# A woven attention loop: the order of TensorE's work written out link by link

## The chip, the cores and the metric

The kernel runs on one core of a Trainium2 chip. The metric is the device time of one execution in microseconds, as the median of several runs. The core has engines that run side by side and synchronise by semaphores: PE (TensorE, matmuls), DVE (VectorE), ACT (ScalarE), POOL (GpSimd) and SP (SyncE, which here only issues DMAs). Each engine works through its own queue in order.

## The reference

Two layers act on `x` of shape (2, 1024, 512). Only the first layer's attention is touched by the change.

```python
xn = layernorm(x)
q, k, v = (silu(causal_dwconv(xn @ W, taps, bias)) for each of q, k, v)   # 16 heads of 128
k = k / sqrt(128)
alpha, beta = sigmoid(xn @ Wa + ba), sigmoid(xn @ Wb + bb)                # one each per head and step
def step(S, (q, k, v, alpha, beta)):                                      # S is 128 x 128 per head
    err = S k - v
    S = alpha * S - beta * err k^T
    return S, S q
o = layernorm(scan(step)) * ln_w + ln_b
s = (o * sigmoid(xn @ Wg)) @ Wo
x = x + s * silu(mlp(xn))
```

The second layer (a gated linear recurrence beside an MLP with 4-bit weights) follows in the same program and is not changed.

## The kernel before, in words

The recurrence is done in chunks of 128 steps. There are 8 groups of two heads (`hg`), and with the batch of 2 a group has `NS` = 4 independent streams. A group has 8 chunks (`c`), taken in pairs (`p`, 256 steps) for the projections.

Inside a chunk the recurrence is a triangular system. Its matrix L comes from k k^T and from the decays; the running sum of the log decays is called g. The system is solved in four blocks of 32 rows, whose diagonal blocks are inverted beforehand.

The first stretch of the program, called the front here, holds a layernorm of `x`, the first layer's MLP (`mlp`, a generator that hands out its work in pieces by `some(n)`), the decays, and for group 0 everything that must be ready ahead of the loop. Then comes the attention loop over groups, pairs and chunks; then the join (`Join`, which multiplies with `Wo`); then the second layer.

The functions of the loop are these:

- `project` does one product with a 512 x 256 weight block: two halves of four 128x512 matmuls each, into PSUM tiles `pwq`, `pwk` or `pwv` of a pool with two buffers. ACT copies each half into `pre` and writes a scaled copy into the destination, DVE adds three taps of the convolution, ACT applies silu.
- `ahead` prepares one pair of the **next** group: the k product, the decay matrix `e` (a DMA that broadcasts rows of g from `gr`, a mask on DVE, four exps on ACT) and k k^T (`pkk`), which DVE multiplies into L (`lt`). k, e and L go to DRAM.
- `invert` inverts the diagonal blocks of the next group in 31 dependent pairs of DVE instructions (`tl`, `ml`); it is a generator too.
- `within` fetches what a chunk needs (L into `ground`, `eb`, and rows of g into `eg`, of which ACT takes the exp), multiplies k and q with it on POOL (`kg`, `qg`), and forms `at` and `kd` from two PE products (`pqk`, and the transpose `pk`).
- `across` is the chain of a chunk. Its links in order: `pks` (state times k) on PE, `rt` on DVE, the transpose `pr` on PE, `rr` on ACT; then four times `pw` on PE, `w4` on ACT, `pz` on PE, `rr` on DVE; then `wt`, the state's product `pst`, the new state on DVE, and the output `po`. After `po` come the statistics of a layernorm on DVE (`st`, `mv`), a power on POOL (`rs`), `nm` on DVE and the scaled output `on` on ACT.
- `finish` transposes `on` of the chunk before (`pot`), scales it (`ot`), multiplies with the gate and stores it.

The pools `eg`, `eb`, `kg`, `qg`, `kb`, `q`, `v` and `gate` have two buffers each, `rr` and `w4` one, the PSUM pools `pi` and `ps` three. In the program's text a pair's three products come first, then for each of its two chunks `within`, `across`, `finish` of the chunk before, and then either `ahead` of the next group (chunks 0 to 3) or nine steps of `invert` (chunks 4 to 7).

The order in which each engine takes its instructions is made when the program is built: a scheduler of the framework places them by their dependencies, by program order as priority and by its own estimate of durations. Nothing in the loop's text fixes it by hand. `issue_after` keeps the loop behind the MLP's last ACT instruction.

Of the kernel before, what the change touches and what calls it, by code (L numbers as in the profile page):

```python
# [17 lines left out]
ALU = mybir.AluOpType  # L18
# [16 lines left out]
NEG = -1.0e30  # L35
EPS = 1e-5
# [16 lines left out]
def cols(ap, n):  # L53

    if len(ap.shape) == 2:
        ap = ap.unsqueeze(2)
    return ap.to_broadcast([ap.shape[0], ap.shape[1], n])

# [154 lines left out]
def first_layer(ctx, tc, a, cst, minus_half, keep, xnT, od, gd, then):  # L213
# [25 lines left out]

    nc = tc.nc  # L240
# [5 lines left out]
    dr = ctx.enter_context(tc.tile_pool(name="at_d", bufs=2, space=DRAM))  # L246
# [59 lines left out]
    nc.sync.dma_start(lnwb, a["lnwb"])  # L306

# [122 lines left out]
    gr = dr.tile([NCOL, P], F32, name="gr", bufs=1)  # L430
    for i in range(NCOL // P):
        pgt = pools["a"].tile([P, P], F32, tag="pa", name=f"pgt_{i}")
        nc.tensor.matmul(pgt, lhsT=sp[:, i * P : (i + 1) * P], rhs=ntriu, start=True, stop=True)
        gt = pa.tile([P, P], F32, tag="lt", name=f"gt_{i}")
        nc.scalar.copy(gt, pgt)
        nc.sync.dma_start(gr[i * P : (i + 1) * P, :], gt)

    def g_rows(hg, c, dst):
        col = c * H * B + hg * NS
        nc.sync.dma_start(  # L440
            dst, gr[col : col + NS, :].rearrange("s t -> (s t)").unsqueeze(0).to_broadcast([P, NS * P])
# [6 lines left out]
    def project(j, n, hg, p, w, dst):  # L448

        u = f"{n}_{hg}_{p}"  # L450
        for hl in range(2):
            h = hg * 2 + hl
            pp = pools["a"].tile([P, B, 2 * P], F32, tag="pa", name=f"p{u}_{hl}")
            for kc in range(KC):
                nc.tensor.matmul(  # L455
# [6 lines left out]
            pre = pools["p"].tile([P, B, 2 * P + 4], F32, tag="pre", name=f"pre{u}_{hl}", bufs=3)  # L462
            if p == 0:
                nc.gpsimd.memset(pre[:, :, 0:3], 0.0)
            else:
                nc.gpsimd.tensor_copy(pre[:, :, 0:3], halo[:, j, hl, :, 0:3])
            nc.scalar.copy(pre[:, :, 3 : 2 * P + 3], pp)
            if p < NC // 2 - 1:
                nc.gpsimd.tensor_copy(halo[:, j, hl, :, 0:3], pre[:, :, 2 * P : 2 * P + 3])
            acc = dst[:, 2 * hl : 2 * hl + 2, :]  # L470
            nc.scalar.activation(  # L471
                acc, pp, AF.Identity, scale=cw[:, j, h, 3:4], bias=cb[:, j, h : h + 1]
            )
            for tap in range(3):
                nc.vector.scalar_tensor_tensor(  # L475
                    acc,
                    in0=pre[:, :, tap : tap + 2 * P],
                    scalar=cw[:, j, h, tap : tap + 1],
                    in1=acc,
                    op0=ALU.mult,  # L480
                    op1=ALU.add,
                )
        nc.scalar.activation(dst, dst, AF.Silu)


    def ahead(hg, p, w, store):
        u = f"{hg}_{p}"
        ka = pa.tile([P, NS, 2 * P], F32, tag="ka", name=f"ka_{u}")
        project(1, "wk", hg, p, w["wk"], ka)
        nc.sync.dma_start(store["k"][p], ka)  # L490
        for c in (2 * p, 2 * p + 1):
            col = c * H * B + hg * NS
            k = ka[:, :, (c % 2) * P : (c % 2 + 1) * P]
# [3 lines left out]
            g_rows(hg, c, e[:, :, 1 : P + 1])  # L497
# [5 lines left out]
            nc.sync.dma_start(store["e"][c], e[:, :, 1 : P + 1])  # L503
            pkk = pools["i"].tile([P, NS, P], F32, tag="pi", name=f"pkk_{hg}_{c}")
            for s in range(NS):
                nc.tensor.matmul(pkk[:, s, :], lhsT=k[:, s, :], rhs=k[:, s, :], start=True, stop=True)
            lt = pa.tile([P, NS, P], F32, tag="lt", name=f"lt_{hg}_{c}")
            nc.vector.tensor_tensor(lt, pkk, e[:, :, 0:P], ALU.mult)
            for bl in range(4):
# [3 lines left out]
                )  # L513

# [33 lines left out]
    def within(hg, c, q, k, v, store):  # L548
# [11 lines left out]
        g_rows(hg, c, eg[:, :, 1 : P + 1])  # L560
        nc.scalar.activation(eg[:, :, 1 : P + 1], eg[:, :, 1 : P + 1], AF.Exp)
# [3 lines left out]
        nc.gpsimd.tensor_tensor(qg, q, eg[:, :, 1 : P + 1], ALU.mult)  # L565

        def four(tag, lhsT, rhs):
            ps = pools["i"].tile([P, NS, P], F32, tag="pi", name=f"{tag}_{u}")
            for s in range(NS):
                nc.tensor.matmul(ps[:, s, :], lhsT=lhsT[:, s, :], rhs=rhs[:, s, :], start=True, stop=True)  # L570
            return ps

        def turned(tag, src):
            ps = pools["i"].tile([P, NS, P], F32, tag="pi", name=f"{tag}_{u}")
            for s in range(NS):
                nc.tensor.transpose(ps[:, s, :], src[:, s, :], ident)
            return ps


        at = pools["b"].tile([P, NS, P], F32, tag="at", name=f"at_{u}")  # L580
        nc.vector.tensor_tensor(at, four("pqk", k, q), e, ALU.mult)
        kd = pools["b"].tile([P, NS, P], F32, tag="kd", name=f"kd_{u}")
        nc.vector.tensor_tensor(kd, turned("pk", k), cols(e[:, :, P - 1 : P], P), ALU.mult)
        return eg, qg, kg, at, kd, v, G

    def across(hg, c, state, parts):

        u = f"{hg}_{c}"
        eg, qg, kg, at, kd, v, G = parts
# [6 lines left out]
        else:  # L596
            pks = pools["s"].tile([P, NS, P], F32, tag="ps", name=f"pks_{u}")
            for s in range(NS):
                nc.tensor.matmul(pks[:, s, :], lhsT=state[:, s, :], rhs=kg[:, s, :], start=True, stop=True)
            nc.vector.tensor_tensor(  # L600
                rv, vv, pks.rearrange("p s (b t) -> p s b t", t=32), ALU.subtract
            )

# [536 lines left out]
```

## Time and profile before

| what | value |
|---|---|
| median of 3 runs | 3361.08 us (3361.02 to 3362.52) |
| the profiled execution's own time | 3359.76 us, span 3357.7 us |
| granted TensorE clock | 0.998 |
| front, up to the first `pwq` | 0 to 324 us |
| attention loop, up to its last `pw` | 324 to 1853 us |
| busy in the loop: PE, DVE, ACT, POOL | 1464, 1066, 1059 and 640 us of 1529 |
| join and second layer | from 1853 us on |

The page of a profile gives busy times, the chain of work that ended last and the costliest groups of instructions. Beside it the trace answers questions: what an engine waited for, what stands in a stretch of time, how one tile was made and used. In a row of groups the columns after the bar are busy time and the mean of one in ns, and after the next bar the engine's idle time just before these instructions, with what ended it. PE records two entries for each fp32 matmul, one for a transpose.

### The profile page before, as it was taken

The numbers are of one execution on the slowest core, as the hardware profiler recorded it, in microseconds if no ns is written. First come the engines' busy times: TensorE is split into PE (matmuls) and PEld (weight loads), VectorE is DVE, ScalarE is ACT, GpSimd is POOL, SyncE is SP. The second block draws the span as 40 slices with busy tenths as digits, with TensorE's granted clock in tenths as the row PEclk, the third lists the DMA queues.
The fourth block names the chain that finished last, engine by engine and source line by source line (L and its number), as shares of the span: only waits on it lengthen the run. The fifth ranks groups of instructions, "written<-read, shape, count | busy, mean of one in ns | idle before, by whom it ended". The sixth has DMA issues, their size and how long they took to land.

```text
span 3357.7 us, 35998 instructions
## 1 busy us (share of the span) xinstructions
PE 3253.2 (97%) x11734; PEld 1803.9 (54%) x11734; DVE 2079.6 (62%) x4397; ACT 1425.9 (42%) x2480; POOL 865.9 (26%) x1520
## 2 busy tenths in 40 slices
PE   8999999999999999999999999999999999999998
PEld 6677565656565665656566444444444444444443
DVE  4445676676867677686855623666666655555545
ACT  3453676767677677767666000222222200110002
POOL 2000334343343435344344200111121100000102
PEclk9999999999999999999999999999999999999999
DMA  5122443434434343433351653111111100000003
GB/s 168 56 73 77 119 122 102 109 86 126 109 87 127 101 108 87 125 105 95 91 141 43 194 153 101 35 32 32 31 32 32 44 25 19 19 23 22 19 0 125
DMA packets 428699, 268.21 MB, mean 80 GB/s; under 512 B 193888, under 2 KB 368480, under 8 KB 428512
## 3 DMA queue, kind: packets, MB, share of 16 engines
q1 hardware_dynamic: 418208, 248.87, 26.2%
q0 software_dynamic: 5696, 8.65, 0.9%
q10 hardware_dynamic: 4608, 8.39, 0.7%
q8 instruction: 94, 1.54, 0.2%
q14 instruction: 93, 0.76, 0.1%
HBM read 179.71 MB, written 86.11 MB: 79 GB/s over the span
## 4 chain that ended last, share of the span: by engine, by line
PE 43%; DVE 6%; ACT 2%; issue 2%; POOL 2%; DMA 0%; POOLq 0%; DVEq 0%; ACTq 0%
PE po L1005 10%; PE jpo L183 6%; PE pgc L928 3%; PE pgd L928 3%; PE puc L928 3%; PE pua L928 3%; PE pga L928 3%; PE pud L928 3%; PE pgb L928 1%; PE pub L928 1%; DVE ga L886 1%; PE pgate L741 1%; PE pwk L455 1%; PE pwv L455 1%; PE pr L871 1%
## 5 line engine op out<-in xcount | busy, mean ns | idle before, releaser
L1005 PE MATMUL po<-w_d,u 128*128 128x512 f32 x1024 | 456.8, 599 | 10.9 <-DVE acc L1016 5.4
L1005 PEld LDWEIGHTS po<-w_d,u 128*128 128x128 f32 x1024 | 190.0, 190 | 272.0 <-issue 207.3
L948 ACT COPY g<-pga 128x512 f32<-128x512 f32 x32 | 18.7, 586 | 640.1 <-PE pga L928 640.1
L629 POOL COPY wt<-w 32x128 f32<-32x128 f32 x512 | 233.2, 456 | 113.4 <-ACT w L624 91.8
L455 PE MATMUL pwq<-xnT,wq 128*128 128x512 f32 x512 | 251.3, 593 | 0.0
L455 PE MATMUL pwv<-xnT,wv 128*128 128x512 f32 x512 | 240.3, 599 | 9.1 <-ACT q L471 8.4
L455 PE MATMUL pwk<-xnT,wk 128*128 128x512 f32 x512 | 247.0, 594 | 0.0
L1016 DVE TENSOR_TENSOR acc<-acc,po 128x512 f32<-128x512 f32 x240 | 163.0, 682 | 135.6 <-PE po L1005 134.5
L741 PE MATMUL pgate<-xnT,wg 128*128 128x512 f32 x512 | 238.8, 593 | 0.1
L183 PE MATMUL jpo<-wo,jo 128*128 128x512 f32 x512 | 225.0, 592 | 0.0
L475 DVE SCALAR_TENSOR_TENSOR ka<-prewk,cw,ka 128x512 f32<-128x512 f32 x192 | 151.2, 788 | 65.4 <-ACT ka L471 54.8
L475 DVE SCALAR_TENSOR_TENSOR q<-prewq,cw,q 128x512 f32<-128x512 f32 x192 | 149.8, 780 | 55.9 <-ACT q L471 53.8
L475 DVE SCALAR_TENSOR_TENSOR v<-prewv,cw,v 128x512 f32<-128x512 f32 x192 | 155.7, 827 | 42.8 <-ACT v L471 40.6
L622 PEld LDWEIGHTS pw<-rr,ground 128*128 128x128 f32 x512 | 88.8, 188 | 169.8 <-DVE rr L621 121.3
L974 ACT ACTIVATE g<-g 128x512 f32<-128x512 f32 x96 | 60.4, 630 | 261.1 <-DVE g L938 260.9
L616 PEld LDWEIGHTS pz<-w,ground 128*128 128x128 f32 x768 | 119.7, 190 | 84.3 <-ACT w L624 51.2
L183 PEld LDWEIGHTS jpo<-wo,jo 128*128 128x128 f32 x512 | 95.0, 191 | 107.1 <-issue 107.1
L616 PE MATMUL pz<-w,ground 128*128 128x128 f32 x768 | 140.7, 283 | 8.0 <-ACT w L624 8.0
L455 PEld LDWEIGHTS pwv<-xnT,wv 128*128 128x128 f32 x512 | 91.3, 191 | 104.9 <-issue 83.4
L832 POOL TENSOR_TENSOR w_g<-w_g 128x256 f32<-128x256 f32 x16 | 11.9, 741 | 503.8 <-DVE w_g L818 503.8
L673 ACT ACTIVATE on<-po,nm,rs 128x128 f32<-128x128 f32 x256 | 96.3, 457 | 107.0 <-DVE nm L668 107.0
L622 PE MATMUL pw<-rr,ground 128*128 128x128 f32 x512 | 107.4, 292 | 31.2 <-DVE rr L621 27.9
(246 smaller groups left out, 6806.6 us busy)
## 6 DMA issues: line engine op xcount, KB each, us to landing
e<-gr SPq DMA_DIRECT2D x64, 256.0 KB, 4.4
de<-e SPq DMA_DIRECT2D x64, 256.0 KB, 2.6
dk<-ka SPq DMA_DIRECT2D x32, 512.0 KB, 2.8
kb<-dk SPq DMA_DIRECT2D x32, 512.0 KB, 4.7
eb<-de SPq DMA_DIRECT2D x64, 256.0 KB, 2.8
eg<-gr SPq DMA_DIRECT2D x64, 256.0 KB, 3.8
od<-ot SPq DMA_DIRECT2D x64, 256.0 KB, 2.1
jo<-od SPq DMA_DIRECT2D x16, 1024.0 KB, 6.4
```

Source lines behind the costliest of these rows:

```text
L183: nc.tensor.matmul(po, lhsT=ot[:, h, :], rhs=self.wo[h], start=(h == 0), stop=(h == H - 1))
L455: nc.tensor.matmul(pp, lhsT=w[:, kc, hl * P : (hl + 1) * P], rhs=xnT[:, kc, :, p * 2 * P : (p + 1) * 2 * P], start=(kc == 0), stop=(kc == ...
L475: nc.vector.scalar_tensor_tensor(acc, in0=pre[:, :, tap : tap + 2 * P], scalar=cw[:, j, h, tap : tap + 1], in1=acc, op0=ALU.mult, op1=ALU.add,
L616: nc.tensor.matmul(pz[:, bl, :], lhsT=G[:, SLOT[bb] + bl - bb, :], rhs=w4[:, bb, :], start=(bb == 0), stop=(bb == bl - 1),)
L622: nc.tensor.matmul(pw[:, bl, :], lhsT=G[:, SLOT[bl], :], rhs=rr[:, bl, :], start=True, stop=True)
L629: nc.gpsimd.tensor_copy(dst, w4[r, bl])
L673: nc.scalar.activation(on[:, s, :], po[:, s, :], AF.Identity, scale=rs[:, s : s + 1], bias=nm[:, s : s + 1])
L741: nc.tensor.matmul(pg, lhsT=w["wg"][:, kc, hl * P : (hl + 1) * P], rhs=xnT[:, kc, :, p * 2 * P : (p + 1) * 2 * P], start=(kc == 0), stop=( ...
L928: nc.tensor.matmul(banks[key], lhsT=w[:, i, par, :], rhs=q[:, j, par, :], start=(first and par == 0), stop=(par == 1), skip_group_check=no ...
L974: nc.scalar.activation(ge[key], x, AF.Gelu_apprx_tanh)
L1005: nc.tensor.matmul(po, lhsT=inter[par, h][:, i * P : (i + 1) * P], rhs=wd[:, par, :], start=(par == 0), stop=(par == 1),)
L1016: nc.vector.tensor_tensor(dst, dst, po, ALU.add)
```

## The change

- `project`, `ahead` (now `ahead_k` and `ahead_l`), `within`, `across`, `finish` and a new `gated` become generators that hand out their work in pieces, with an amount of PE time for each piece (`WIDE`, `NARROW`, `TURN`).
- `weave` takes a chunk's chain in nine links. After each link it hands out other pieces until a fixed share (`SHARES`) of the others' total has been given. The chain is emitted at a higher priority for the scheduler.
- `mm` and `turn` keep PE's instructions of the loop in the order of the program's text.
- k and L are prepared two groups ahead of the chunk at hand instead of one. The front now also does this for group 1, and the loop begins with the products of the first pair and `within` of the first chunk.
- Beside a chunk stand now the products of the following pair: q and k in its even chunk, v and gate in its odd one; `within` of the next chunk; `finish` of the last one, which now includes the layernorm's statistics; and five pieces of `invert`.
- The gate's sigmoid becomes a tanh of half the argument plus one; the missing factor of one half goes into `lnwb`.
- exp(g) is computed once, in the front, and stored to DRAM as `egr`; `within` fetches its rows from there instead of taking the exp per chunk.
- The weights of the next group are loaded one pair before they are used.

The core of the diff:

```diff
+HIGH = 200
+WIDE, NARROW, TURN = 0.86, 0.22, 0.11
+SHARES = (0.17, 0.29, 0.39, 0.49, 0.58, 0.67, 0.76, 0.85, 0.97)
...
-    dr = ctx.enter_context(tc.tile_pool(name="at_d", bufs=2, space=DRAM))
+    dr = ctx.enter_context(tc.tile_pool(name="at_d", bufs=3, space=DRAM))
...
+    nc.vector.tensor_scalar(lnwb, lnwb, 0.5, None, ALU.mult)
...
         nc.sync.dma_start(gr[i * P : (i + 1) * P, :], gt)
+        egt = pa.tile([P, P], F32, tag="lt", name=f"egt_{i}")
+        nc.scalar.activation(egt, pgt, AF.Exp)
+        nc.sync.dma_start(egr[i * P : (i + 1) * P, :], egt)
...
+    def mm(out, **kw):
+        i = nc.tensor.matmul(out, **kw)
+        if "b" in pools:
+            tc.keep_in_program_order(i)
...
+    def gated(hg, p, w, gate):
+        for cost, ready in wide(f"pgate_{hg}_{p}", hg, p, w):
+            if ready:
+                hl, pg = ready
+                part = gate[:, 2 * hl : 2 * hl + 2, :]
+                nc.scalar.activation(part, pg, AF.Tanh, scale=0.5)
+                nc.scalar.activation(part, part, AF.Identity, bias=1.0)
+            yield cost
...
         nc.gpsimd.memset(eg[:, :, 0:1], 1.0)
-        g_rows(hg, c, eg[:, :, 1 : P + 1])
-        nc.scalar.activation(eg[:, :, 1 : P + 1], eg[:, :, 1 : P + 1], AF.Exp)
+        rows(egr, hg, c, eg[:, :, 1 : P + 1])
...
-    wk = load_weights(0, ("wk",))
-    store = new_store(0)
     for p in range(NP):
-        some(IC // 2)
-        ahead(0, p, wk, store)
-    for _ in invert(0, store):
+        some(3)
+        done(ahead(0, p, wk, stores[0]))
+    wk = load_weights(1, ("wk",))
+    for i, _ in enumerate(invert(0, stores[0])):
         some(1)
+        if i % 6 == 1 and i // 6 < NP:
+            done(ahead(1, i // 6, wk, stores[1]))
...
+    def weave(chain, others):
+        total = sum(cost for cost, _ in others)
+        others = itertools.chain.from_iterable(steps for _, steps in others)
+        given = 0
+        while True:
+            with tc.high_priority(HIGH):
+                share = next(chain, None)
+            if share is None:
+                break
+            while given < share * total:
+                cost = next(others, total)
+                given += cost or 0
+        done(others)
...
+                if c % 2 == 0:
...
+                    plan = (
+                        (pot, 1, 0), (ready, 1, 0), (steps, 2, 0), (wide_q, None, 8 * WIDE), (pot, None, 4 * TURN), (steps, 2, 0),
+                        (wide_k, KC, 4 * WIDE), (ready, 1, 4 * TURN), (steps, 1, 0),
+                        (wide_k, None, 4 * WIDE), (ready, None, 4 * NARROW),
+                    )
+                else:
...
+                    plan = (
+                        (pot, 1, 0), (ready, 1, 0), (ls, 1, 0), (steps, 2, 0), (wide_v, None, 8 * WIDE), (pot, None, 4 * TURN),
+                        (steps, 2, 0), (ls, 1, 4 * NARROW), (gates, KC, 4 * WIDE),
+                        (ls, None, 4 * NARROW),
+                        (ready, 1, 4 * TURN), (steps, 1, 0), (gates, None, 4 * WIDE),
+                        (ready, None, 4 * NARROW),
+                    )
...
+                weave(across(hg, c, state), others)
```

In a `plan` each entry is a generator, how many of its pieces are taken, and their PE time. `pot` is `finish` of the chunk before, `ready` is `within` of the next chunk, `steps` is `invert`, `ls` is `ahead_l`. The `yield SHARES[n]` in `across` stand after `pks` and its `rt`, after `pr` with its `rr`, and then after each `pw` with its copies and each `pz` with its `rr`.

## The prediction

> **What bounds the kernel now.** I read the busy table first, then the stretches of one head group, then PE's waits, then the timeline where they gather.
>
> ```profile
> PE 3253.2 (97%) x11734; PEld 1803.9 (54%) x11734; DVE 2079.6 (62%) x4397; ACT 1425.9 (42%) x2480; POOL 865.9 (26%) x1520
> ```
>
> PE looks full, but its ends are modelled, so I count starts. In the timeline 16 records of pgate run from 1036.25 to 1043.12: 0.43 us each, two records per 128x512 matmul, so 0.86 us; a 128x128 matmul comes to 0.22 us and a transpose to 0.11. A head group issues 128 wide matmuls (four products of 8 for each of 4 pairs), 34 x 8 - 12 = 260 narrow ones (chunk 0 has no pks and no qg part in po, chunk 7 no pst) and 96 transposes: 110.1 + 57.9 + 10.6, about 178.5 us. Counted from first pr to first pr, a group takes 194.9 (741.3 to 936.2). So about 16 us of each group is PE waiting. Over the loop (324 to 1853) I sum start-to-start excess to about 125 us; that is the ceiling of any gain.
>
> Where in a group? The stretches are chunks 0, 1, 2, then 4, 5 and 6; columns: span, then busy of PE, PEld, DVE, ACT, POOL.
>
> ```profile
> 741.30:762.00 20.70, 20.65 (x108) 13.93 (x107) 12.66 (x32) 13.04 (x28) 10.10 (x20) 1.00 0.23 66
> ...
> 796.50:812.40 15.90, 15.90 (x81) 10.61 (x81) 9.43 (x27) 10.45 (x23) 8.31 (x16) 1.00 0.30 76
> ...
> 852.00:870.70 18.70, 17.68 (x87) 11.41 (x87) 16.82 (x48) 10.29 (x24) 6.26 (x13) 1.00 0.51 140
> 870.70:896.40 25.70, 22.10 (x110) 13.73 (x108) 23.51 (x59) 20.76 (x37) 11.15 (x17) 1.00 0.40 117
> 896.40:916.70 20.30, 17.84 (x85) 11.08 (x86) 17.85 (x48) 10.79 (x19) 9.20 (x17) 1.00 0.32 81
> ```
>
> PE's issue work between the same points is 16.6, 20.3 and 16.3 in chunks 4 to 6, so they lose 2.1 + 5.4 + 4.0 = 11.5 of the 16. These are the chunks that hold `invert`, and DVE is busy 88 to 91% of them. The other five lose about 4.5 together. Who is waited for (us, times, longest; window 480 to 1660):
>
> ```profile
> PE pw L622 <- DVE rr L621: 24.4, 33, 1.4
> PE pz L616 <- ACT w L624: 5.4, 6, 1.0
> PE pr L606 <- DVE rt L600: 5.1, 6, 0.8
> ```
>
> And why rr is late: it stands in DVE's queue behind inversion steps (tl, ml).
>
> ```profile
> 1073.46 1.20 DVE L538 TENSOR_TENSOR ml<-ml,tl 128x255 f32<-128x255 f32 x1
> 1074.69 0.42 DVE L531 TENSOR_TENSOR tl<-ll,ml 128x256 f32<-128x256 f32 x1
> 1075.03 0.28 DVE L621 TENSOR_TENSOR rr<-rr,pz 128x128 f32<-128x128 f32 x1
> ```
>
> So the bound is PE's issue work plus queue delay on in-order DVE and ACT. With a free engine a link is short: from the last pz record to the end of rr 0.49 us, from pw to the end of w4 0.47, each plus 0.06 to PE.
>
> **What the Trainium skill says.** "Trainium Kernel Development and Optimization", section Performance Expectations, calls matmul busy time a bad metric because matmuls are pipelined: agreed, 97% busy hides 125 us. "Perfetto Trace Analysis", Optimization Strategy, says that interleaving regimes with different contended engines may help; here the regimes are the PE-bound and the DVE-heavy chunks above. "ScalarE activation tables: per-element evaluation and per-set limits", What a function is on this engine, puts two functions of different sets one table load of 1283 ns apart: the trace has 1283. "DMA: Bandwidth & Descriptors", Anatomy of one DMA, says that a DMA's semaphore wait happens on the issuing sequencer and that completion latency dominates; its fit (for GpSimd's path) gives 2.0 + 0.6 us for 256 KB. The trace shows 3.8 for the eg load below, and I use that.
>
> **The change part by part.** I use the compiled order of both programs beside the durations of the trace.
>
> *Even cover.* PE's order in the loop is now fixed. In groups 0 to 5 the compiled order leaves 1.1 to 2.6 us of other work between two links (0.86 at one of them in odd chunks) where before it was mostly 0.86, and pks to pr has 3.44. Alone this would hide a link of 0.55 us with a tap (0.7) ahead of it. PE's count is unchanged.
>
> *Table loads.* Gate by tanh, egr ready-made: loads in the loop fall from 224 to about 75.
>
> ```profile
> L483 ACT ACT_TABLE_LOAD x85 | 109.1, 1283 | 1.5
> ...
> L748 ACT ACT_TABLE_LOAD x55 | 70.6, 1283 | 1.0
> ...
> L561 ACT ACT_TABLE_LOAD x43 | 55.2, 1283 | 7.6 <-DMA eg<-gr 6.9
> L500 ACT ACT_TABLE_LOAD x41 | 52.6, 1283 | 0.7
> ```
>
> ACT loses 150 x 1.28 = 192 us and 64 x 0.64 = 41 of exp, and gains 64 Identity passes at about 0.6 = 38. ACT is only 69% busy in the loop; what this saves PE is w4 waits, inside the walk below. The two extra exps and stores for egr are once, behind the MLP: nothing.
>
> *Inversion.* Its 62 steps a group no longer stand in chunks 4 to 6: the compiled DVE order has 26 in chunk 1 and 28 in chunk 2, 8 in chunk 0. Pricing each row of DVE's order (tap 0.79, step 0.41, at/kd/lt/rt/e 0.68, wt 0.29, state 0.30, st and mv 0.44) and scaling by 0.92, which brings the same sum for chunks 4 to 6 of before to its measured busy time, chunks 1 and 2 hold 25.6 and 25.5 us of DVE work against 23.5 and 21.8 us of PE work. DVE is the bound of these two.
>
> *The eg load ahead of rs.* `within` for chunk c+1 now issues while chunk c starts. Its eg buffer is free after state(c-1), so memset, load, kg, qg follow at the start of chunk c, just when rs of chunk c-1 (POOL's power) is due. In chunks 2 and 5 POOL's order has kg ahead of rs, in chunk 3 kg and qg.
>
> ```profile
> L563 POOL TENSOR_TENSOR kg<-kb,eg x64: 1261/1272/1733, 337.6 to 1828.6; 128x512 f32<-128x512 f32 x64
> L565 POOL TENSOR_TENSOR qg<-q,eg x64: 1083/1134/1637, 341.9 to 1829.8; 128x512 f32<-128x512 f32 x64
> ...
> DMA to landing us min/median/max: 3.1/3.8/5.5
> ```
>
> The wait is new in its place: rs stands in POOL's queue behind kg, which waits for the load; nm on DVE waits for rs with steps and taps queued behind it; on waits for nm with prewq, rr and the conv copy queued behind it; pr's successor pw waits for rr. Walk chunk 2, pks at 0: state done -0.3, eg landed 3.6, kg 4.9, rs (1.0) 6.0, nm 6.4, four on 8.0. ACT's order has on and then prewq (0.6) ahead of rr: rr at 8.9. PE wants it at 0.89 + 3.44 + 0.44 + 1.72 = 6.5: 2.4 us lost. Chunk 3, with qg and a state that ends 0.6 in: on ends near 9.8, then v's 0.8 and w4 (0.3): 10.9 against 8.4, 2.5 lost. Chunk 5 has kg only: 0.7. SP holds the load behind four ground loads (0.6 each), which are through by then. Before, rs always stood ahead of kg, so the trace shows no such wait; its bounds are 0 (the load lands before bn is through) and 3.5 a chunk (landing at 5.5). I take the walk.
>
> *Sum for a group* (us over issue work): chunk 0 0.8; chunk 1 3 (the walk gives 1.8, 1.10 x DVE's work gives 4.7); chunk 2 5.5 (4.5 to 6.4: steps, the late rr, then rr behind taps); chunk 3 2.5; chunk 4 1.7 (a table load and exps ahead of w4); chunks 5, 6, 7 0.7, 0.4, 0.2; 0.2 in each for what no walk sees, 1.6. That is 16.4, against 16.1 before (mean of groups 1 to 5): +0.3 x 5 = **+1.5**.
>
> *Group 0.* `invert` of group 1 is now at the loop's start: DVE's order puts all 62 steps, 15 taps and four wider rows ahead of the first rr, 40.3 x 0.92 = 37 us that start some 3 us in; PE wants that rr about 35 us after the first wide matmul (pr 29 us after it as now, then 6): +5; its chunks 1 and 2 have no steps. 16 against 14.5: **+1.5**.
>
> *Groups 6 and 7* have no k product two groups ahead, so in their even chunks links have 0.86 us of cover, and 26 to 33 steps fall into chunk 1 of group 6 (25.5 us of DVE on 20.0 of PE). Group 6: 16 against 191.0 - 176.8 = 14.2, **+2**. Group 7: chunk 6 has nothing between its links where before the join's matmuls stood, about 6 us; in all 15 against 10, **+5**.
>
> *Front.* k and L of group 1 (34.6 us of PE) move there; the total is unchanged, and PE is 99% busy from 100 to 300. ACT takes 28 us and some 8 loads more, beside MLP work: **+3** (0 to 8). Weights of the next group load a pair earlier; SP carries the same transfers: nothing, hidden behind a chunk of slack.
>
> Total +13 on the profiled execution's 3359.8 (span 3357.7 and 2.1 around it); the median of the runs stands 1.3 above it: **3374 us**. By the same terms the likeliest case's own range is 3350 to 3398. About 0.2% (6.7 us) is what a measurement can tell from no change.
>
> **Rivals.**
> - *Cover wins, faster.* The late rs and the bunched steps cost little because 1.72 us of cover absorbs them: 8 us left per group. For it: free latencies of 0.5 us, a fifth less ACT work. Against it: an in-order queue passes its delay on. 6 x -8 + 5 for groups 6, 7 and front = -43: 3318. It decides as soon as chunks 2 and 3 lose under 1.5 us each.
> - *DVE bound in full, slower still.* Chunks 1 and 2 last 1.10 times DVE's work (28.2, 28.0: 10.9 lost), as chunks 4 to 6 do now, and on comes late in more chunks: 22 per group, +36, groups 6 and 7 +15, front +3: 3414.
> - *It doesn't do what it says.* Other engines' order follows the scheduler, and loss only moves from chunks 4 to 6 to chunks 1 to 3: no change, 3361.
>
> **How the numbers follow.** Forecast 0.45, faster 0.25, slower still 0.2, no change 0.1. The forecast's spread puts a tenth of it below 3361 and a quarter within 0.2%. Slower 0.55, same 0.16, faster 0.29. The range 3312 to 3422 leaves out about a tenth on the fast side and under a tenth on the slow.
>
> **What would show it.** Right: groups of 1 to 5 near 195 us; chunks 1 and 2 longest over their issue work; waits of PE on rr (ACT) and w4 in chunks 2 and 3 with on just ahead; POOL's kg idle on the eg load ahead of rs; table loads near 133 in all; fewer waits of pw on rr in chunks 4 to 6. Wrong: groups under 188 us, or on running before prewq without delaying rr.

## The result, and the profile after

The changed kernel takes 3436.4 us (median of 4 runs, 3433.5 to 3438.0) against 3361.1 (4 runs): a ratio of 1.0224, 95% interval 1.0206 to 1.0242. The profiled execution took 3435.1 with a span of 3433.3, so 75.6 us more span than before. The sign of the forecast was right; its size (13 us) was far too small.

The busy table of the page after. The counts on PE are the same, ACT does 192 us less, and PE's share falls from 97 to 95%:

```profile
PE 3266.4 (95%) x11734; PEld 1817.2 (53%) x11734; DVE 2086.8 (61%) x4398; ACT 1233.9 (36%) x2345; POOL 868.3 (25%) x1520
```

I measure stages as the prediction did, from first pr to first pr. Where PE's work differs (34.6 us of k and L of one group moved to the front: 32.8 out of group 6 and 1.8 out of group 5), I compare the loss over issue work.

| stage | before | after | more |
|---|---|---|---|
| start to first pr | 353.2 | 394.2, of it 34.6 moved in | 6.4 |
| group 0 | 193.1 | 196.9 | 3.9 |
| groups 1 to 5 | 973.0 | 1006.0, with 1.8 less work | 34.8 |
| group 6, loss | 14.2 | 170.6 - 144.0 = 26.6 | 12.4 |
| group 7 and the rest (difference to the span) | | | 18.1 |

The stretches of after, chunks 2, 3 and 5 of some groups; columns: span, busy of PE, PEld, DVE, ACT, POOL, then the granted clock, DMA share and GB/s.

```profile
666.72:693.49 26.77, 24.07 (x122) 15.67 (x120) 13.92 (x34) 10.20 (x23) 11.99 (x21) 1.00 0.39 96
...
717.81:745.36 27.55, 25.43 (x121) 17.38 (x120) 13.33 (x34) 13.40 (x30) 10.86 (x19) 0.94 0.38 114
...
840.06:867.69 27.63, 23.93 (x106) 14.82 (x105) 24.13 (x62) 15.94 (x30) 10.96 (x21) 0.94 0.28 76
...
919.84:946.43 26.59, 24.07 (x122) 15.67 (x120) 13.82 (x34) 13.18 (x30) 10.87 (x18) 1.00 0.38 113
...
1242.68:1270.03 27.35, 22.55 (x106) 13.79 (x105) 24.27 (x62) 15.74 (x30) 11.08 (x21) 1.00 0.28 78
1270.03:1297.99 27.96, 25.44 (x121) 17.12 (x120) 13.81 (x33) 10.42 (x23) 11.76 (x21) 0.94 0.37 94
```

Two things stand here. Chunk 2 (840.06) takes 27.6 us for 21.8 of issue work. And there is a number that before read 1.00 in every such row: the **granted clock**, 0.94 in some. The page's PEclk row rounds it away. In the trace, the clock changes only at steps of 3.41 us. Cut at these steps, chunk 2 of group 2 (840.06) and chunk 2 of group 4 (1242.68) show what decides:

```profile
840.24:843.65 3.41, 2.14 (x8) 0.83 (x6) 0.85 (x1) 0.00 (x0) 3.11 (x3) 1.00 0.34 102
843.65:847.06 3.41, 0.98 (x4) 0.71 (x5) 3.24 (x9) 3.18 (x9) 0.82 (x2) 1.00 0.00 0
847.06:850.48 3.42, 3.42 (x10) 2.00 (x9) 3.39 (x9) 2.43 (x8) 2.42 (x6) 0.50 0.23 69
```

```profile
1243.00:1246.42 3.42, 2.00 (x7) 0.69 (x5) 1.38 (x3) 0.33 (x1) 3.03 (x3) 1.00 0.34 102
1246.42:1249.83 3.41, 1.54 (x5) 0.90 (x6) 3.27 (x8) 3.41 (x11) 0.65 (x1) 1.00 0.00 0
1249.83:1253.24 3.41, 3.00 (x14) 1.62 (x13) 3.38 (x9) 2.91 (x9) 2.97 (x7) 1.00 0.29 84
```

In the first, PE stands still for 3.70 us; 2.43 us of it fall into one step, and the next step runs at half clock: four pwq records take 2.96 us there instead of 1.88. In the second, PE stands still for 3.29 us, but the grid of steps cuts this into 1.42 and 1.87, and the clock stays full. Summed over such steps (1 minus the clock), the loop loses 34.1 us of clock after and 1.7 before.

Lost clock is not lost time. The order of the instructions in groups 1 to 4 is the same on PE, DVE, ACT and POOL, so their chunks can be compared. Chunk 2 takes 27.35 us without a dip (group 4) and 27.37, 27.54 and 27.63 with one: hardly any difference. Chunk 3 takes 26.45 and 26.77 without and 27.78 and 27.97 with one; chunk 5 takes 26.24 to 26.59 without and 27.55 with one. So a dip costs about 0.2 us in chunk 2 and 1.2 in chunks 3 and 5. By these differences I estimate that the half clock is some 10 of the 34.8 us of groups 1 to 5.

The waits of PE in groups 0 to 5 (us, times, longest):

```profile
PE pw L467 <- ACT rr L668: 30.9, 18, 3.7
PE pz L467 <- ACT w L685: 27.4, 17, 2.5
PE pw L467 <- DVE rr L681: 17.7, 29, 1.8
```

The first two are new: before, PE waited 5.4 us for ACT's w in the like window, and for ACT's rr hardly at all. The chain of waits of after, cut to chunk 2 of group 2, tells why in one column:

```profile
835.98 4.40 DMA eg<-egr
840.40 0.04 POOLq L624
840.45 0.09 issue
840.54 1.27 POOL kg L624
841.80 0.97 POOL rs L733
842.80 1.06 DVE nm L735
843.92 0.32 issue
844.24 1.15 ACT on L740 x3
845.38 0.48 ACT prewq L503
845.86 0.17 ACT rr L668
846.04 0.04 issue
846.08 0.49 PE pw L467 x2
```

That is the walk of the prediction, step by step: eg lands, kg, rs, nm, on, prewq, rr, pw. From the moment its input is ready until it starts, rs now takes 2.6, 3.0 and 2.9 us in chunks 2, 3 and 5 (medians of groups 1 to 5); before, these medians were at most 0.2 in every chunk. On the page the idle time of ACT ahead of on is now 262 us (107 before):

```profile
L740 ACT ACTIVATE on<-po,nm,rs 128x128 f32<-128x128 f32 x256 | 99.6, 460 | 262.3 <-DVE nm L735 261.9
```

POOL's kg answers to the row of before: the landing median rose from 3.8 to 4.2 us, and POOL's idle time ahead of kg now ends with the eg load:

```profile
L624 POOL TENSOR_TENSOR kg<-kb,eg x64: 1261/1267/1802, 375.4 to 1892.4; 128x512 f32<-128x512 f32 x64
...
  DMA eg<-egr: 74.9, 38
...
DMA to landing us min/median/max: 3.1/4.2/6.0
```

And of ACT's table loads in the loop, two groups are left, from 391 to 1921 us 59 loads in all:

```profile
L520 ACT ACT_TABLE_LOAD x30 | 38.5, 1283 | 0.5
L552 ACT ACT_TABLE_LOAD x29 | 37.2, 1283 | 0.5
```

### The profile page after: what moved, and what is told of

Its sections match the earlier page's. It is cut to its first block, busy times and chain, and to the rows that moved or that the text cites. A ratio compares the mean times of both kernels' runs of the same rounds, so it can differ in the third digit from the quotient of the medians.

```text
span 3433.3 us, 35758 instructions
## 1 busy us (share of the span) xinstructions
PE 3266.4 (95%) x11734; PEld 1817.2 (53%) x11734; DVE 2086.8 (61%) x4398; ACT 1233.9 (36%) x2345; POOL 868.3 (25%) x1520
## 4 chain that ended last, share of the span: by engine, by line
PE 59%; DVE 20%; ACT 7%; issue 4%; DMA 4%; POOL 4%; SPq 1%; POOLq 0%; DVEq 0%; ACTq 0%
PE po L1130 10%; PE jpo L193 5%; PE pgate L467 4%; PE pwq L467 3%; PE pgc L1053 3%; PE pgd L1053 3%; PE puc L1053 3%; PE pua L1053 3%; PE pga L1053 3%; PE pud L1053 3%; DVE q L511 2%; DVE ka L511 2%; DMA eg<-egr 2%; PE pwk L467 2%; PE po L374 2%
## 5 line engine op out<-in xcount | busy, mean ns | idle before, releaser
L1130 PE MATMUL po<-w_d,u 128*128 128x512 f32 x1024 | 456.8, 599 | 10.9 <-DVE acc L1141 5.4
L690 POOL COPY wt<-w 32x128 f32<-32x128 f32 x512 | 250.6, 489 | 127.9 <-ACT w L685 105.6
L467 PE MATMUL pgate<-xnT,wg 128*128 128x512 f32 x512 | 255.6, 603 | 2.6 <-ACT v L507 2.6
L511 DVE SCALAR_TENSOR_TENSOR v<-prewv,cw,v 128x512 f32<-128x512 f32 x192 | 162.8, 856 | 73.4 <-ACT v L507 71.1
L511 DVE SCALAR_TENSOR_TENSOR q<-prewq,cw,q 128x512 f32<-128x512 f32 x192 | 169.6, 883 | 53.7 <-ACT q L507 50.4
L467 PE MATMUL pz<-w,ground 128*128 128x128 f32 x768 | 125.1, 286 | 35.0 <-ACT w L685 35.0
```

What stands on the lines that cost most here:

```text
L467: i = nc.tensor.matmul(out, **kw)
L511: nc.vector.scalar_tensor_tensor(acc, in0=pre[:, :, tap : tap + 2 * P], scalar=cw[:, j, h, tap : tap + 1], in1=acc, op0=ALU.mult, op1=ALU.add,
L690: nc.gpsimd.tensor_copy(dst, w4[r, bl])
L1130: nc.tensor.matmul(po, lhsT=inter[par, h][:, i * P : (i + 1) * P], rhs=wd[:, par, :], start=(par == 0), stop=(par == 1),)
```

## Experiments

Times are medians; the kernel before took 3359 to 3361 beside them. "Clock" is the sum of lost clock over the loop, worked out as above.

**1. rs ahead of kg and qg.** `last["rs"]` holds the newest power; both products get an order edge behind it.

```diff
+        for i in (a, b) if "rs" in last else ():      # a = kg, b = qg
+            tc.add_manual_dep(i.ins, last["rs"].ins.name, NoSync)
```

> The changed kernel with kg and qg of a chunk queued on POOL behind the newest rs (the power of the chunk before), order only. Theory 'late rs' (rs stands behind kg, which waits for the eg load; nm, on, rr and w4 inherit it): in chunk 2 of a group nm starts about 1.5 us earlier, the wait of pw on ACT's rr falls from 3.7 to about 1.4 us, the waits in chunks 3 and 5 mostly go, and with them the stretches of half clock behind them; 8 to 10 us a group in groups 1 to 5 and a few us in the others, so about 55 us less than the changed kernel: 3380 us (3365 to 3400). Rival 'DVE bunch' (the 54 inversion steps of chunks 1 and 2 set the time, rs or not): chunk 2 stays over 26.5 us, under 20 us gained, 3417 us or more.

3408.1 (1.0139, 1.0124 to 1.0154): 28 less than the changed kernel, half of what was expected, and between the two theories. Groups 1 to 5 fall from 201.2 to 197.1. The waits show what happened:

```profile
PE pw L467 <- DVE rr L687: 31.5, 42, 1.8
PE pw L467 <- ACT rr L674: 22.1, 24, 1.5
PE pz L467 <- ACT w L691: 14.8, 26, 1.1
```

ACT's two waits fall by 21 us, DVE's grows by 14, no wait is over 2.0 us, and rs starts 0.08 us after its input. The clock sum falls from 34.1 to 8.5 and is zero in groups 1 to 5. So late rs is shown as the cause of the long waits.

Why only half of the gain? Over groups 1 to 5, chunks 2 to 7 together become 33 us shorter, but chunks 0 and 1 become 13 us longer. There kg had run long before rs was due and did no harm. The edge now puts kg right behind rs, beside nm, and nm takes 1.22 us instead of 0.16 (last section). What is gained in chunks 2 to 7 is partly clock, partly the waits themselves: chunk 2 is 1.4 us shorter than the one of the changed kernel that ran at full clock (25.96 on average against 27.35).

**2. Idle time filled.**

```diff
+            if bl == 0 and c == 2:          # 8 times at bl == 1 in chunks 3 and 5
+                for _ in range(12):
+                    mm(pw[:, 3, :], lhsT=ident, rhs=ident, start=True, stop=True)
```

> The changed kernel with PE work that nobody reads: 12 128x128 matmuls (2.6 us) ahead of the first pw in each chunk 2, and 8 (1.8 us) ahead of the first pz in each chunk 3 and 5, into a part of pw that is written over later. They stand where PE idles 3.1 to 3.7 and 2.1 to 2.5 us in groups 1 to 5. Theory 'clock' (an idle stretch of PE over about 2 us brings some 3.4 us at half clock, 1.7 us lost, and that is part of the price of a stall): PE does 180 us more of bare issue work over the eight groups' 24 places at 0.22 us each, at most 45 us in all and nearly all of it inside the idle time, and still the kernel gets faster, since some 11 half-clock stretches of groups 1 to 5 go: 15 to 20 us less, 3417 us. Rival (the lower clock in the record costs nothing beyond the stall): no gain, 3436 to 3445 us.

3495.8 (1.0402), 59 more instead of 15 to 20 less. The bare work is 8 x 28 x 0.22 = 49 us (the "180" in the expectation is a slip). The filled place itself lost its dip: the 24 records ran 861.20 to 864.04 at full clock and rr was then 0.82 us late instead of 3.70. But the queues came out in another order, with more DVE work ahead of later links: in the same chunk the next pw waits 3.79 us for DVE's rr. The clock sum is still 30.7. So the run is no test of what the clock costs, one way or the other.

**3, 16. The tanh part alone, in the kernel before,** whole (gate and exp once), then exp once only (the last two lines, and egr stored beside gr).

```diff
-                    nc.scalar.activation(gate[:, 2 * hl : 2 * hl + 2, :], pg, AF.Sigmoid)
+                    nc.scalar.activation(part, pg, AF.Tanh, scale=0.5)
+                    nc.scalar.activation(part, part, AF.Identity, bias=1.0)
...
-        nc.scalar.activation(eg[:, :, 1 : P + 1], eg[:, :, 1 : P + 1], AF.Exp)
+        g_rows(hg, c, eg[:, :, 1 : P + 1], egr)      # egr instead of gr
```

> The kernel before with one part of the change: gate by tanh with an Identity pass, and exp(g) stored once and loaded ready-made, nothing else. Theory: ACT loses some 150 table loads (192 us) and 64 exps, PE gains only what waited for ACT in the loop: 0 to 15 us less than before, 3346 to 3361 us. Rival (this part carries some of the loss, since the longer ACT chain of two passes delays gate or frees its PSUM later): 3366 us or more.

> The kernel before with exp(g) stored once and loaded ready-made, the gate by Sigmoid as before. The whole tanh part made it 35 us slower. Theory (eg that the scheduler holds early ready is what moves the other engines' order; the loads that tanh saves are a gain): 3385 to 3400 us, as with the whole part. Rival (the gate of two passes carries it): 3355 to 3370 us.

3396.0 (1.0099, 1.0082 to 1.0115) and 3384.1 (1.0070, 1.0055 to 1.0085). A net saving on ACT slows the kernel by 35 us, and 23 of these come with exp once (the theory of run 16 asked for 3385 to 3400). PE's waits of the whole part, 360 to 1760 us, have a new first line:

```profile
PE pk L579 <- DVE at L584: 18.7, 7, 2.7
```

It was 3.8 us, longest 0.6, before; and the clock sum is 25.6 (18.8 with exp once). The late rs of the changed kernel stands in both traces too: kg is ahead of rs in chunks 3 and 5, and rs starts 1.4 and 2.3 us after its input there (0.1 before). So eg, which is ready without an exp on ACT, moves POOL's order in the old program as well. Groups 1 to 5, however, hold only 21 of the 35 us and 7 of the 23; no run separates the rest.

**4. PE's order left free.**

```diff
     def mm(out, **kw):
-        i = nc.tensor.matmul(out, **kw)
-        if "b" in pools:
-            tc.keep_in_program_order(i)
+        nc.tensor.matmul(out, **kw)          # turn likewise
```

> The changed kernel with the same program text, but PE's instructions left to the scheduler instead of kept in program order. Theory 'late rs': POOL's order still has kg ahead of rs in chunks 1, 2 and 5, so rr and w4 stay late, and the even cover is gone: 3410 to 3450 us. Rival 'fixed PE order' (PE waits in line at links where the scheduler would have put other work first): the loss goes with the order, 3361 us or less.

3468.1 (1.0318), clock sum 42.7: 32 more than with the order held, beyond the expected range. So the fixed order of PE is not what costs. How much it saves by itself is not shown, since the other queues came out in another order too.

**5, 9, 12. The tanh part undone under the weave:** both halves, exp once only, and both with rs first.

```diff
-        rows(egr, hg, c, eg[:, :, 1 : P + 1])
+        rows(gr, hg, c, eg[:, :, 1 : P + 1])
+        nc.scalar.activation(eg[:, :, 1 : P + 1], eg[:, :, 1 : P + 1], AF.Exp)
...
-                nc.scalar.activation(part, pg, AF.Tanh, scale=0.5)
-                nc.scalar.activation(part, part, AF.Identity, bias=1.0)
+                nc.scalar.activation(part, pg, AF.Sigmoid)
```

> The changed kernel without one part: the gate is Sigmoid again and exp(g) is taken in every chunk, all else as changed (PE's order in the loop is pinned, so the weave stays). Theory: under the woven order the tanh part is a gain, since ACT then does some 150 table loads (190 us) and 64 exps less; without it w4 and rr come later and the kernel takes 10 to 40 us more, 3446 to 3476 us. Rival (the tanh part carries a third to half of the loss here too, as when it was made alone): 3400 us or less.

> The changed kernel with exp(g) taken in every chunk again, the gate still by tanh. Its POOL order is the one of the run with both undone: rs of chunk 2 ahead of kg of chunk 4's neighbour where the changed kernel has kg first, since the scheduler holds eg later ready. Theory (what made the undone tanh part a gain is this order of rs and kg, not the loads): 3405 to 3418 us, as with both undone or a little less, as ACT keeps the saved loads. Rival (the Identity pass and the tanh gate cost it): over 3428 us.

> kg and qg behind rs and the tanh part undone, both of which alone took about 25 us off the changed kernel. Theory (both worked through rs ahead of kg): together no more than one of them, 3400 to 3412 us. Rival (they are separate losses): 3380 to 3390 us.

3412.4, 3416.0 and 3427.2. Run 9 came as its theory said; runs 5 and 12 fell outside both of their theories. The chunks tell why (mean length in groups 1 to 5, us):

| chunk | 0 | 1 | 2 | 3 | 4 | 5 | 6 | 7 |
|---|---|---|---|---|---|---|---|---|
| changed kernel | 22.7 | 25.6 | 27.6 | 27.3 | 24.4 | 26.8 | 22.2 | 24.6 |
| 1, rs first | 23.6 | 27.3 | 26.0 | 24.9 | 23.9 | 25.6 | 22.1 | 23.8 |
| 5, both undone | 22.7 | 25.6 | 25.9 | 25.2 | 24.4 | 24.8 | 26.6 | 23.5 |
| 9, exp once undone | 22.7 | 25.6 | 26.0 | 25.2 | 24.4 | 24.8 | 26.7 | 23.6 |
| 12, 5 with rs first | 23.5 | 27.3 | 25.9 | 25.2 | 24.4 | 24.8 | 26.1 | 24.1 |

- *Order of rs and kg.* In runs 5 and 9 POOL's order in the trace has kg behind rs in chunks 2, 3 and 5, where the changed kernel has it ahead; rs starts 0.08 us after its input, and these chunks are 1.7, 2.1 and 2.0 us shorter.
- *The exp.* Taken in every chunk, it waits in ACT's queue for the eg load, with prewq, q and w queued behind it. Chunk 6 is 4.4 us longer, and for 2.1 to 2.4 us of it PE waits at pz for this w. In run 12:

```profile
747.74 0.64 ACT L621 ACTIVATE eg<-eg 128x512 f32<-128x512 f32 x1 [2.85 <-DMA eg<-gr]
```

- *The table loads.* Run 9 has 71 loads fewer than run 5 (189 against 260) and is no faster. So the loads that the gate's tanh saves are worth nothing to PE here.
- *The edge of run 1.* Where rs is early anyway, it only costs: run 12 differs from run 5 in chunks 0, 1 and 7, where nm now meets kg, by 0.8, 1.7 and 0.6 us a group.

From this an estimate: run 5 with chunk 6 as in the changed kernel would take 194.3 us a group, where the kernel before takes 194.6 with 0.4 more work. So in groups 1 to 5 the loss of the change is about what the order of kg and rs costs. No run has rs first in chunks 2, 3 and 5 alone.

**6, 7. DVE, then DVE, POOL and ACT, held in the order of the text** (each instruction of a chunk gets an order edge behind the one before on its engine).

```diff
                 weave(across(hg, c, state), others)
+                in_order(nc.cur_bb.bb.instructions[traced:], engines)
```

> The changed kernel with DVE's instructions of each chunk held in the order of the text, as PE's are: 10 inversion steps in each of chunks 1 to 5, none bunched (26 and 28 before in chunks 1 and 2). POOL and ACT stay free, POOL still with kg ahead of rs in several chunks. Theory 'DVE bunch': pw's waits on DVE's rr (24 us in groups 0 to 5) go and chunk 2 gets shorter by 2 us; late rs stays: 3400 to 3425 us. Rival (bunching is harmless, and DVE held in order waits for POOL's rs with everything queued behind nm): 3436 us or more.

> The changed kernel with DVE, POOL and ACT all held in the order of the text within the loop: rs right behind bn and ahead of memset, kg and qg, on right behind nm, the inversion in fives, rr and w4 at their links. Theory (the loss is what the scheduler made of the three free queues, not PE's fixed order): groups 1 to 5 under 190 us, no half clock in them, 3320 to 3361 us. Rival (held in order, ACT waits at on for nm, and POOL at kg for the eg load, with halo copies, wt and prewq queued behind): groups over 197 us, 3400 us or more.

3889.0 (1.157) and 3813.4 (1.135): both far worse. The first line of PE's waits in each, 360 to 1760 us:

```profile
PE pw L467 <- DVE rr L681: 195.1, 63, 5.0
```

```profile
PE pw L467 <- ACT rr L668: 126.8, 43, 4.9
```

In the text, taps stand right behind their product and wait for ACT's pass, and eight exps stand ahead of rr; in order, rr waits with them. The scheduler's orders of the side queues are far better than the text's. That they carry the loss because they leave the text, my theory for run 7, is refuted.

**8, 10. Cover in the last groups:** half of the gate product moved to even chunks in groups 6 and 7; then, with rs first, the last pair's gate product held back from chunk 5 to chunk 6 of group 7.

```diff
+                        # run 8: in groups 6 and 7 the first KC steps of gated() go into the even chunk's plan
+                        gates = gated(...) if hg + 2 < HG else split
...
+                        # run 10
+                        if following == windows[-1]:
+                            held, gates = gates, none      # given out in chunk 6
```

> The changed kernel with half of the gate product moved from odd to even chunks in groups 6 and 7 (even chunks there 12 wide matmuls' worth of cover units instead of 8 and odd 12 instead of 16; the work is the same). Theory 'thin cover' (the two last groups lose 26 and 27 us because their even chunks have 0.86 us between links): 5 to 10 us less than the changed kernel, 3426 to 3431 us. Rival (their loss comes from late on and rr, from inversion steps in group 6, and from chunk 6 of group 7 where nothing is left to put between): within 3 us of 3436.

> kg and qg behind rs, and the gate product of the last pair (16 wide records twice, 6.9 us of PE) moved from chunk 5 to chunk 6 of group 7, where nothing stands between the links. Compared with kg and qg behind rs alone (3408). Theory 'no cover' (chunk 6 of group 7 takes 21 us for 10.6 us of issue work, half of what group 7 loses): chunk 6 stays near 21 with 6.9 us more in it, chunk 5 gets 5 to 7 us shorter: 3400 to 3404 us. Rival (the time is lost to late on and rr whatever stands between): chunk 6 grows by 6 and nothing is gained, 3406 us or more.

3430.6 (6 less) and 3401.1 (7 less than rs first). In the former group 7 gains 6.2 to the pr of its last chunk (145.8 to 139.6) and group 6 loses 3.4. In the latter chunk 6 takes 20.6 us with 6.9 us more work in it (21.0 without); chunk 5 falls from 21.3 to 18.5, less than the 5 to 7 us that were expected of it, and chunk 4 from 19.0 to 17.3. Missing cover is shown for chunk 6 of group 7.

**11, 13, 14, 15. SHARES, inversion steps spread, and sums.** SHARES moved to (0.17, 0.33, 0.43, 0.53, 0.60, 0.70, 0.77, 0.85, 0.97); the spread holds only the tl multiply of each step in place:

```diff
+            if "b" in pools:
+                tc.keep_in_program_order(first)      # first = the tl multiply
```

> kg and qg behind rs, and SHARES moved so that the links have the cover where they wait: in odd chunks 2.58 us ahead of the first pw (1.72), 2.19 ahead of the first pz (1.72), 1.75 ahead of the third pw (0.86). In kg and qg behind rs alone (3408) the waits at these three in groups 0 to 5 sum to 25, 19 and 32 us. Theory (stalls are latency less cover, link by link): 10 to 25 us less, 3383 to 3398 us. Rival (the late engine is behind by queued work, so a later link only moves the wait along): within 5 us of 3408.

> kg and qg behind rs, and of each inversion step only the tl multiply held at its place in the text (all else on DVE free): 10 and 14 steps in chunks 1 and 2 instead of 26 and 28, the rest over chunks 3 to 7. Compared with kg and qg behind rs alone (3408, where chunks 1 and 2 last 27.3 and 25.9 us for 23.5 and 21.8 of issue work and DVE's rr holds PE some 8 us a group). Theory 'DVE bunch': chunks 1 and 2 get 4 us shorter together and the others at most 2 longer: 3390 to 3400 us. Rival (a step that is pinned waits and holds up DVE wherever it stands, as when all of DVE was held in order): 3410 us or more.

> The three parts together that made the changed kernel faster: kg and qg behind rs, the moved SHARES, the last gate product in chunk 6 of group 7. Theory (they act in different places): 28 + 6 + 7 less than 3436, 3395 us (3390 to 3400), still over the kernel before. Rival (the moved shares and rs work on the same waits): 3400 us or more.

> The same three parts and the inversion steps spread as in the first kernel of this call. Theory 'DVE bunch': 8 to 18 us less than the three parts, 3377 to 3387 us. Rival (pinned steps hold up DVE): no gain on the three parts, 3395 us or more. By neither is the kernel before (3360) reached.

Shares with rs first 3401.9, 6 less, between the two theories; spread with rs first 3419.5, 11 **more**, against the bunch theory; three parts 3395.0, as added up; four parts 3374.3 (1.0044, 1.0027 to 1.0061), 21 less than three and better than either theory. So spreading the steps pays only together with the moved shares: by itself it takes chunk 2 from 25.9 to 23.0 us, but chunks 3 and 6 lose 2.4 and 3.7. Groups 1, 2 and 6 of the four-part kernel, in the stretches:

```profile
582.60:775.40 192.80, 184.52 (x873) 117.30 (x872) 147.65 (x335) 111.56 (x232) 84.58 (x157) 1.00 0.39 107
775.40:968.00 192.60, 185.03 (x873) 117.62 (x872) 146.45 (x335) 111.43 (x232) 84.44 (x157) 1.00 0.40 108
...
1545.00:1713.70 168.70, 152.47 (x745) 98.30 (x744) 120.33 (x294) 75.86 (x170) 76.38 (x132) 1.00 0.30 83
```

At 192.5 on average, groups 1 to 5 are 2.1 us **faster** than before (194.6; 0.4 of it is work moved to the front), at full clock. Over the span it is still 15.0 slower: start 1.9, groups 0 to 5 -9.0 for the same work, group 6 10.5 (168.7 - 144.0 against 14.2 lost), the rest 11.6. What remains is the two groups without a k product.

**17, 18. Shares from measured latencies, and the balance in group 7 alone,** on the four parts: 

```diff
-SHARES = (0.17, 0.33, 0.43, 0.53, 0.60, 0.70, 0.77, 0.85, 0.97)
+SHARES = (0.145, 0.32, 0.43, 0.58, 0.63, 0.76, 0.82, 0.87, 0.97)
...
+                    split = hg == HG - 1 and following and following != windows[-1]      # run 18
+                    if split:
+                        wide_k = split = gated(*following, w["wg"], nxt[3])
```

> The four parts, with SHARES set link by link from the latencies of the four-part run: 0.86 us of cover taken from pks to pr (3.44, latency at most 1.7) and from the fourth rr to pw (1.72, latency 0.5), and given to the first pw (2.58 and 3.44 us) and to the third (2.16 and 2.19). There the waits at the first pw, second and third pw were 2.8, 1.9 and 2.2 us a group. Theory (stall is latency less cover): 3 to 5 us less a group, 3350 to 3362 us, the kernel before's time or just under. Rival (queued work only moves along): 3370 us or more.

> The kernel just before, and half of the gate product moved to even chunks in group 7 alone, where the balanced run won 6 us (139.6 instead of 145.8 from the first pr of group 7 to that of its last chunk) while it lost 3 in group 6. Theory (thin cover): 3 to 6 us less than the kernel just before. Rival: no difference.

3403.4 (1.0126) and 3407.1 (1.0140): 29 worse than four parts, and no gain from the balance. In groups 1 to 5, the wait at the third pw went from 1.3 us a group to nothing, the one at the first pw only from 2.3 to 1.7. But in odd chunks the second w now comes up to 2.3 us late, 8.2 us a group, and the clock sum rises from zero to 20.5 (29.0 in run 18). ACT's timeline of one of them:

```profile
620.55 1.06 ACT L520 ACTIVATE v<-v 128x1024 f32<-128x1024 f32 x1 [3.90 <-DVE v L511]
621.51 0.25 ACT L693 COPY w<-pw 128x128 f32<-128x128 f32 x1
```

The link was moved up a little, and w now stands behind the Silu of v, which waits 3.9 us for DVE's last tap. The rival was right: here w is late by what is queued ahead of it, not by a latency that a share can be cut to. No version beat the kernel before.

## Why the prediction was right or wrong

- **"Sum for a group" (the step that failed).** It gave 16.4 us of loss over issue work; 23.0 was measured. Late rs is 5.6 of the forecast (2.4, 2.5 and 0.7), so everything else was put at 10.8, 5 us less than before the change. This saving did not come: without late rs (run 5, with chunk 6 as in the changed kernel) 16.1 is lost by the estimate above, as before. By chunk, 0 to 7, measured: 1.9, 2.1, 5.8, 3.8, 2.6, 3.3, 0.4, 3.2; forecast: 0.8, 3, 5.5, 2.5, 1.7, 0.7, 0.4, 0.2 and 1.6 unplaced. The error lies in the odd chunks 3, 5 and 7, with 10.3 measured and 3.4 forecast. Besides late rs they were put at nothing, though each has one link with only 0.86 us of cover, less than the 0.55 + 0.7 us of a link with a tap ahead of it: at this third pw, PE waits 1.4, 0.6 and 1.2 us for DVE's rr even in run 5.
- **Late rs (right in mechanism, place and sum).** In chunk 2 of group 2 POOL sat 4.42 us ahead of kg for the eg load, then came rs, nm, on, rr as walked. On the scale of the walk, with pks at 0, eg landed at 4.7 instead of 3.6, and nm took 1.04 us instead of 0.4, as qg ran beside it; so 3.7 us were lost at this wait where 2.4 were walked. In chunk 5 PE waited 2.1 us where the walk gave 0.7. Against run 5, chunks 2, 3 and 5 cost 1.7, 2.1 and 2.0 us: 5.8 together, 5.6 forecast. That the sum fits so well is partly luck, as the chunks don't. "Before, rs always stood ahead of kg" is not so: in the trace of before, kg runs ahead of rs in chunks 0, 1 and 7, but so early that rs starts at most 0.7 us after its input.
- **Half clock (no term).** No part of the prediction has it: 20.5 us of clock lost in groups 1 to 5, worth some 10 us by the estimate above. The trace of before could have warned: its one dip of the loop stage (at 334) follows a pause of 2.16 us at 331, and no later pause is over 1.7.
- **Inversion on DVE (half right).** 26 and 28 steps do stand in chunks 1 and 2, but DVE sat 3.69 us idle ahead of nm in chunk 2 and was busy 24.1 of 27.6: not the bound in full. Run 13 shows that bunching alone is no loss to be undone; run 15 that it is one once the shares are moved.
- **ACT's savings (right size, right to expect little).** 133 loads are left in all, as forecast, and ACT does 192 us less (195 forecast). The loads of the gate bring PE nothing (runs 5 and 9). Exp once makes chunk 6 shorter by 4.4 us a group, and by what it does to POOL's order costs more than that (undone in run 9, 20 us are gained).
- **Groups 6 and 7 (mis-sized).** +2 and +5 forecast, 12.4 and 18.1 measured; 8.5 us of clock are lost in them. Chunk 6 of group 7 loses about 11 (22.1 for 10.6 of work), not 6; chunks 4 and 6 of group 6 lose 2.0 us each at the first rr.
- **Front and start.** +3 forecast for the front, 2.4 measured (361.2 - 324.2 - 34.6); loop start and group 0: +1.5 forecast, 4.0 + 3.9 measured.
- **Even cover.** The links stand as counted, with free links at 0.47 and 0.49. The thin link is the one told above.
- **Rivals.** "Slower still" came nearest (3414). Its first half fails: chunks 1 and 2 lose 7.9 us together, not 10.9, and DVE does not bound them in full. Its second half, on late in more chunks, is what the trace shows. "Cover wins" needed chunks 2 and 3 to lose under 1.5 us each; they lost 5.8 and 3.7. Its idea is borne out only in the four-part kernel, in groups 0 to 5. The third, that loss only moves between chunks, does not hold for the change as a whole, which lost more than it moved; it describes run 13.

By steps, forecast and measured: front 3 and 2.4, start and group 0 1.5 and 7.9, groups 1 to 5 1.5 and 34.8, group 6 2 and 12.4, the end 5 and 18.1: 13 and 75.6. What stays open: how much of group 6's 12 is cover and how much the inversion of group 7, since the balanced run moved both; what makes up the 7.9 of start and group 0; and what a half-clock stretch costs by itself, which no run isolates.

## What to carry to other kernels

Where a scheduler orders the other queues, price a change by the compiled order of every engine, not by the instructions saved: an operand made ready earlier can be put ahead of an urgent short instruction, and then waits there for its load. Put the urgent instruction first only where it is late: an order edge that holds everywhere can put a long POOL product beside the next short DVE instruction (run 1). Short waits of TensorE cost their own length; once 2 us of idle fall into one step of its clock's grid, half clock can come on top. And look at the last passes of a pipelined loop, where the work that covers others has run out.

## What the runs showed of the hardware

- **2 us of idle within one 3.41 us step bring half clock.** The Trainium skill, "TensorE: Matmul & The Clock Gate", Part 1, "What's actually happening", says that TensorE falls to half rate after an idle window of about 3.4 us and needs about as long of work to come back, in a window that runs freely. The traces agree on the length and on the grid: in each of the twenty traces all changes of the clock between 300 and 3300 us, 740 in all, lie within 1% of a whole number of 3.41 us steps of each other. But the step need not be idle throughout. Over the loops of all traces, none of 8382 full-clock steps with less than 1.4 us of idle was followed by half clock, 42 of 257 with 1.4 to 2.0 us, and 249 of 250 with 2.0 us or more. So the place of a pause on the grid decides: 23 pauses of 2.5 to 3.3 us that the grid cut into parts under 1.9 us were followed by none.
- **A POOL product stops DVE.** "SBUF — State Buffer", Who interferes with whom, says that VectorE and GpSimd share a port pair as an exclusive lock. The traces agree: at the same place, chunk 1 of group 2, nm takes 0.16 us in the changed kernel with no product beside it, and 1.22 us beside kg in the run with rs first. There 48 of the 64 nm meet kg or qg, in the changed kernel 19.

```profile
814.72 1.01 POOL L733 TENSOR_TENSOR rs<-rs,minus_half 128x4 f32<-128x4 f32 x1 [1.71 <-DVE rs L732]
815.76 0.16 DVE L735 SCALAR_TENSOR_TENSOR nm<-mv,rs 128x4 f32<-128x4 f32 x1 [0.92 <-POOL rs L733]
```

```profile
808.43 1.01 POOL L739 TENSOR_TENSOR rs<-rs,minus_half 128x4 f32<-128x4 f32 x1 [1.71 <-DVE rs L738]
809.40 1.27 POOL L624 TENSOR_TENSOR kg<-kb,eg 128x512 f32<-128x512 f32 x1
809.47 1.22 DVE L741 SCALAR_TENSOR_TENSOR nm<-mv,rs 128x4 f32<-128x4 f32 x1 [0.92 <-POOL rs L739]
```
